# Softmax weights of a graph attention kept in PSUM for the products with values, and copied to SBUF by ScalarE

## The chip, the cores and the metric

The kernel runs on one core of a Trainium2 chip. The metric is device time in microseconds (us) of one execution; the time of a kernel is the median of several executions. A profile is taken of one further execution.

The engines are named as the profile names them: PE is TensorE (PEld its weight loads), DVE is VectorE, ACT is ScalarE, POOL is GpSimd, SP is SyncE.

## The reference, cut to what matters

The reference is two layers of a graph transformer on 3125 nodes and 100000 edges, sorted by destination. The change touches only the graph attention of the first layer:

```python
def _L0_gnn_ref(h, efeat, src, dst, Wq, Wk, Wv, W1, b1, W2, b2, Wo, bo):
    Q = (h @ Wq).reshape(n, H, HD)      # n = 3125 nodes, H = 8 heads, HD = 32
    K = (h @ Wk).reshape(n, H, HD)
    V = (h @ Wv).reshape(n, H, HD)
    score = jnp.einsum('ehd,ehd->eh', Q[dst], K[src]) / np.sqrt(HD)
    score = score + jax.nn.relu(efeat @ W1 + b1) @ W2 + b2
    m = jax.ops.segment_max(score, dst, num_segments=n)
    ex = jnp.exp(score - m[dst])
    denom = jax.ops.segment_sum(ex, dst, num_segments=n)
    alpha = ex / denom[dst]
    out = jax.ops.segment_sum(alpha[:, :, None] * V[src], dst, num_segments=n)
    return out.reshape(n, D) @ Wo + bo
```

The kernel subtracts a running maximum per head instead of the maximum per node, sums `ex * V[src]` and `ex` itself by destination, and divides at the end. Around it stand a dense mixer, a mixture of experts, a second graph layer, a second mixer and a feed-forward part, none of which is touched.

## The kernel before

**Tiling.** The 100000 edges are cut into 40 groups (`NG`) of 2500: four runs (`NR`) of five columns (`KB`) with 125 edges each, one edge per partition. So one group has 20 columns (`GT`). Each run has a buffer `KV` of 125 partitions, five columns and 521 floats per column: 256 for the keys, 256 for the values, eight for the weights `ex`, one constant 1. There are ten such buffers, used in turn, so that the gathers can run up to two and a half groups ahead.

**One group, in the order of the program.**

- POOL gathers the rows of `kv_tab` by source node, one indirect DMA for each column, 20 in a group (L901). SP loads the features of the edges two groups ahead, and the queries and codes of the group after.
- TensorE spreads the queries over the edges by a one-hot product, `qe` (L911). VectorE multiplies keys with it, in place (L914), and sums over each head to `sc` (reductions, L924). This is done for the first pair of runs (`z` = 0) and then for the second. Between these matmuls stand the hidden layer of the edge features of the next group (L783, evacuated by ScalarE at L785) and the output projection of the group before (L845 to L858).
- VectorE adds the bias of the edge features (L926) and finds the maximum: a reduction (L929), a transpose on TensorE (L934), a reduction (L936), a small matmul (L940), and the running maximum `top` (L942). It subtracts it (L944). Between the two matmuls TensorE does the scores of the next group (L796) into the PSUM tile `score`, which ScalarE copies out (L799), and counts (L835).
- ScalarE writes the exponentials into the last columns of each `KV` (L948), VectorE multiplies the values with them, in place (L950), and TensorE sums values and weights by destination, with a one-hot matrix `oh` as weights (L953):

```python
for z in range(2):
    for r in range(2 * z, 2 * z + 2):
        ex = kvs[r][:, :, 2 * D:2 * D + H]
        nc.scalar.activation(ex, sc[:, r * KB:(r + 1) * KB, :], AF.Exp)                                # L948
        v = kvs[r][:, :, D:2 * D].rearrange("p g (h d) -> p g h d", d=HD)
        nc.vector.tensor_tensor(v, v, ex[:, :, :, None].to_broadcast([P, KB, H, HD]), ALU.mult)        # L950
    for i in range(KB):
        for r in range(2 * z, 2 * z + 2):
            pe(nc.tensor.matmul(seg[r * W:(r + 1) * W, :], oh[:, r * KB + i, :], kvs[r][:, i, D:], ...))  # L953
```

  The four runs have four strips of 32 partitions of one PSUM tile `seg`.
- ScalarE copies `seg` to SBUF as `u` (L715), a matmul moves its rows to their window (L719), and ScalarE copies the result as `U` (L971). VectorE adds what the group before carried over (L958 to L975, with an exponential of eight elements at L961) and divides (L979 to L988). TensorE turns the features of the group after the next (L772, copied out by ScalarE at L774), and the next group begins.

**What sets the order.** Every matmul of this stage is tied to the one before by `pe(...)`, so TensorE runs in the order of the program. On the other engines the tile framework orders by priorities and by the dependencies between tiles. It places the waits: an instruction waits for the engines that last wrote or used its tiles. On VectorE the one-hot matrix `oh` of the next group (L697) comes right after the four products, and it waits for the segment sums.

**PSUM.** The eight banks are all in use in this stage: two for `tr` (small transposes and matmuls), two for `hidden`, two for `qe`, one for `score` and one for `seg`.

Of the kernel before, what the change touches and what calls it, by code (L numbers as in the profile page):

```python
# [9 lines left out]
F32 = mybir.dt.float32  # L10
BF16 = mybir.dt.bfloat16
I32 = mybir.dt.int32
AF = mybir.ActivationFunctionType
# [4 lines left out]
N, E, D, H, FE = 3125, 100000, 256, 8, 64  # L18
HD = D // H
P, T = 125, 25  # L20
# [14 lines left out]
NG, NR, KB = 40, 4, 5  # L35
GT = NR * KB
# [41 lines left out]
def kernel(ctx: ExitStack, tc: tile.TileContext, a, out):  # L78
    nc = tc.nc
# [37 lines left out]
    def row(t, shape):  # L117
        return t[:, None, :].to_broadcast(shape)
# [603 lines left out]
    with tc.tile_pool(name="l1", bufs=1) as l1, tc.tile_pool(name="l2", bufs=2) as l2, \  # L722
# [30 lines left out]
        def pe(x):  # L753

            if before[0] is not None:
                tc.add_manual_dep(x.ins, before[0], NOSYNC, reason="order of matmuls")
            before[0] = x.ins.name
# [117 lines left out]
        for g in range(NG):  # L875
# [15 lines left out]
            sc = l2.tile([P, GT, H], F32, name="sc")  # L891
            kvs = []
# [49 lines left out]
            nc.vector.tensor_max(top, old, tps[:, :H])  # L942
            tops.append(top)
            nc.vector.tensor_sub(sc, sc, row(top[:P], [P, GT, H]))  # L944
            for z in range(2):
                for r in range(2 * z, 2 * z + 2):
                    ex = kvs[r][:, :, 2 * D:2 * D + H]
                    nc.scalar.activation(ex, sc[:, r * KB:(r + 1) * KB, :], AF.Exp)  # L948
                    v = kvs[r][:, :, D:2 * D].rearrange("p g (h d) -> p g h d", d=HD)
                    nc.vector.tensor_tensor(v, v, ex[:, :, :, None].to_broadcast([P, KB, H, HD]), ALU.mult)  # L950
                for i in range(KB):
                    for r in range(2 * z, 2 * z + 2):
                        pe(nc.tensor.matmul(seg[r * W:(r + 1) * W, :], oh[:, r * KB + i, :], kvs[r][:, i, D:],  # L953
                                            start=i == 0, stop=i == KB - 1))
# [64 lines left out]
    with tc.If(nc.values_load(flag[0:1, 0:1], min_val=0, max_val=1)):  # L1019
        with tc.tile_pool(name="qp", bufs=1) as qp:  # L1020
# [171 lines left out]
            with tc.tile_pool(name="y1", bufs=1) as l1, tc.tile_pool(name="y2", bufs=2) as l2, \  # L1192
# [14 lines left out]
                with tc.For_i(0, n, 1):  # L1207
                    bi = block_indices(l2, step)
                    nc.vector.tensor_scalar_add(step, step, 1.0)
                    for t in range(T):  # L1210
# [12 lines left out]
                        sc = l2.tile([P, G, H], F32, name="sc")  # L1223
# [11 lines left out]
                        ex = l2.tile([P, G, H], F32, name="ex")  # L1235
# [70 lines left out]
    with tc.tile_pool(name="f1", bufs=1) as f1, tc.tile_pool(name="f2", bufs=2) as f2, \  # L1306
# [96 lines left out]
        for e in range(NE):  # L1403
# [20 lines left out]
            for (s0, ns), xe in zip(SUB, xes):  # L1424
# [8 lines left out]
                r = f2.tile([128, D], F32, name="yr", bufs=3)  # L1433
# [23 lines left out]
    with tc.tile_pool(name="m1", bufs=1) as m1, tc.tile_pool(name="m2", bufs=2) as m2, \  # L1457
# [3 lines left out]
        for g in range(0, T, 5):  # L1461
            r = slice(g, g + 5)
# [86 lines left out]
    with tc.tile_pool(name="h1", bufs=1) as h1, tc.tile_pool(name="h2", bufs=2) as h2, \  # L1549
# [245 lines left out]
        def small(name, dt=F32, shape=(128, 1)):  # L1795
            return h1.tile(list(shape), dt, name=name)

        digits = [(25, 128), (18, 128), (11, 128), (4, 128), (0, 16)]
        part = small("part", I32)
# [74 lines left out]
        for g in range(5):  # L1874
            r = slice(5 * g, 5 * g + 5)
# [47 lines left out]
```

## Time and profile before

| | us |
|---|---|
| median of 3 runs | 2893.51 (2891.22 to 2893.81) |
| the profiled execution: time | 2897.13 |
| the profiled execution: span, first to last instruction | 2895.3 |
| stage of the edge groups, first product (L950) to the end of its work | about 416 to 1706 |

In the stage from 416 to 1706 us, of 1290 us, the engines are busy:

| engine | us |
|---|---|
| PE | 1000.67 |
| DVE | 966.17 |
| ACT | 448.68 |
| POOL | 1014.11 |

The granted clock of TensorE is 0.91 of full speed in this stage, and the DMA engines are busy for 0.81 of it, at 186 GB/s.

How to read it: a group of instructions is given by line, engine, operation and tiles (out<-in), with its count, its busy time, the mean of one in ns, the idle time of the engine just before it, and what ended most of that idle time. In a timeline, equal neighbours are merged (x4), start and length are in us, and the brackets hold idle time and what ended it. PEclk is the share of full speed that the throttle granted to TensorE. No engine is busy for the whole of the stage, so the busy times alone do not say what sets the pace.

### The profile page before, as it was taken

What the parts mean: (1) busy time and instruction counts of PE and PEld (TensorE: products, weight loads), DVE (VectorE), ACT (ScalarE), POOL (GpSimd) and SP (SyncE); (2) the same over time, 40 slices, a digit from 0 to 9 for tenths busy, and PEclk for the clock granted to TensorE, in tenths of its full rate; (3) what the DMA queues carried; (4) which work ended last, traced back from release to release, by engine and by line L of the source; (5) the groups of instructions that cost most, each with busy time, mean ns of one, the idle gap of its engine ahead of it and who ended that gap; (6) DMA issues with size and microseconds to landing.
All of it is one profiled execution on the core that took longest, in us unless ns stands there. A gap on an engine that the chain in (4) does not pass through costs nothing. (4 is left out here: it accounts for less than half of the span.)

```text
span 2895.3 us, 40359 instructions
## 1 busy us (share of the span) xinstructions
PE 2240.8 (77%) x14013; PEld 1404.5 (49%) x14013; DVE 1875.0 (65%) x4137; ACT 934.7 (32%) x1838; POOL 1364.6 (47%) x1172
## 2 busy tenths in 40 slices
PE   2588777777777777787777744799689999978894
PEld 1244434444444444444444323465457775756673
DVE  4748337777777777777777658343478844846446
ACT  0243133333333333333333304212163323243331
POOL 3444368888888887788888712211100002221110
PEclk9788869999998999989999866899899999999997
DMA  7740488888888888888888842233200002000001
GB/s 187 159 126 17 109 192 191 183 193 190 188 193 190 187 195 187 190 188 189 191 194 191 184 111 85 79 98 105 55 2 5 5 1 70 2 1 1 1 19 48
DMA packets 272347, 340.23 MB, mean 118 GB/s; under 512 B 156170, under 2 KB 203437, under 8 KB 271534
## 3 DMA queue, kind: packets, MB, share of 16 engines
q0 software_dynamic: 185600, 219.53, 33.4%
q1 hardware_dynamic: 72794, 101.95, 13.5%
q10 hardware_dynamic: 13732, 16.01, 2.2%
q8 instruction: 114, 1.87, 0.3%
q14 instruction: 107, 0.88, 0.1%
HBM read 294.80 MB, written 43.25 MB: 117 GB/s over the span
## 5 line engine op out<-in xcount | busy, mean ns | idle before, releaser
L901 POOL DMA_INDIRECT KV<-kv_tab,srcs x800 | 1077.4, 1347 | 330.2 <-issue 148.9
L914 DVE TENSOR_TENSOR KV<-KV,qe 125x512 f32<-125x512 f32 (+1 forms) x480 | 266.3, 595 | 154.9 <-PE qe L911 142.9
L953 PE MATMUL seg<-KV,oh 125*32 125x265 f32 x1600 | 267.6, 525 | 126.3 <-DVE KV L950 115.6
L785 ACT ACTIVATE hid<-hidden,b1e 128x910 f32<-128x910 f32 (+1 forms) x240 | 249.5, 1039 | 304.0 <-PE hidden L783 304.0
L911 PE MATMUL qe<-q,ohT 64*125 64x256 bf16 x2400 | 220.2, 280 | 98.5 <-DVE KV L914 95.5
L911 PEld LDWEIGHTS <-ohT 64*125 64x125 bf16 x2400 | 159.7, 134 | 218.3 <-issue 210.8
L783 PE MATMUL hidden<-efT,w1e 64*128 64x455 f32 (+1 forms) x960 | 240.3, 574 | 16.1 <-ACT hid L785 14.7
L953 PEld LDWEIGHTS seg<-KV,oh 125*32 125x32 f32 x1600 | 133.0, 143 | 244.7 <-DVE KV L950 160.8
L924 DVE TENSOR_REDUCE sc<-KV 125x40 f32<-125x1280 f32 x160 | 229.9, 1478 | 0.0
L950 DVE TENSOR_TENSOR KV<-KV 125x1280 f32<-125x1280 f32 x160 | 227.9, 1487 | 1.5 <-ACT KV L948 1.4
L1493 PE MATMUL sum<-adj,f 125*128 125x400 bf16 (+1 forms) x1050 | 197.2, 328 | 0.0
L1295 PE MATMUL build<-oc,op 128*125 128x200 bf16 x1176 | 144.0, 262 | 55.9 <-ACT xn L214 41.4
L192 DVE TENSOR_TENSOR op<-values,ends_of 128x756 bf16<-128x756 bf16 x196 | 108.3, 553 | 93.4 <-PE build L1295 91.5
L1295 PEld LDWEIGHTS <-op 128*125 128x125 bf16 x1176 | 125.8, 144 | 82.3 <-ACT xn L214 41.5
L1493 PEld LDWEIGHTS <-f 125*128 125x128 bf16 x1200 | 115.7, 98 | 102.9 <-issue 31.2
L192 DVE TENSOR_TENSOR oc<-values,ends_of 128x1200 bf16<-128x1200 bf16 x196 | 152.3, 777 | 0.0
L1562 POOL DMA_DIRECT2D ln_cols<-in_L_mix_ln_g_dram x1 | 0.8, 787 | 316.3 <-DVEq L1513 316.3
L1298 ACT ACTIVATE adj<-build 125x400 bf16<-125x400 f32 x171 | 86.0, 504 | 186.0 <-PE build L1295 186.0
L715 ACT ACTIVATE u<-seg 128x265 f32<-128x265 f32 x40 | 15.7, 393 | 332.3 <-PE seg L953 332.3
L1619 PE MATMUL mm<-bt,fw 128*128 128x250 f32 (+1 forms) x416 | 100.8, 405 | 26.4 <-DVE bt L110 23.3
L265 PE MATMUL mm<-bt,w 128*128 128x489 f32 x256 | 110.5, 582 | 5.1 <-ACT bt L112 3.3
L265 PE MATMUL mm<-w,hT 128*128 128x256 f32 (+1 forms) x512 | 112.6, 379 | 0.0
(462 smaller groups left out, 3910.4 us busy)
## 6 DMA issues: line engine op xcount, KB each, us to landing
EF<-in_edge_attr_dram SPq DMA_DIRECT2D x40, 625.0 KB
w<-in_L_ffn_w_dram SPq DMA_DIRECT2D x16, 1024.0 KB
KV<-kv_tab,srcs POOLq DMA_INDIRECT x800
q<-q_tab SPq DMA_DIRECT2D x160, 48.0 KB
dlb<-dl_tab SPq DMA_DIRECT2D x160, 39.1 KB
kv_tab<-kvt SPq DMA_DIRECT2D x25, 224.0 KB
o_tab<-ow SPq DMA_DIRECT2D x40, 128.0 KB
q_tab<-q SPq DMA_DIRECT2D x25, 168.0 KB
```

Source lines behind the costliest of these rows:

```text
L192: nc.vector.tensor_tensor(dst.rearrange("p n (m o) -> p n m o", o=2), values.rearrange("p (u m o) -> p u m o", u=1, o=2).to_broadcast([dst ...
L265: nc.tensor.matmul(o, l, r, start=i == 0, stop=i == len(pairs) - 1)
L783: pe(nc.tensor.matmul(ps[:, s, :n * F2], w1e[f, c * 128:(c + 1) * 128], efTs[g][f, p0:p0 + n, :], start=True, stop=True))
L785: nc.scalar.activation(hids[g][:, c, p0:p0 + n, :].rearrange("h p (f s) -> h s p f", s=2), ps[:, :, :n * F2].rearrange("h s (p f) -> h s p ...
L901: nc.gpsimd.indirect_dma_start(out=kv[:, i, :2 * D], out_offset=None, in_=kv_tab, in_offset=indirect(srcs[:, e:e + 1]))
L911: pe(nc.tensor.matmul(ps[:, i, :], ohT[w, z, (i0 + i) * P:(i0 + i + 1) * P], q3[w, z, k, :], start=k == 0, stop=k == 2))
L914: nc.vector.tensor_mul(kv[:, i0:i0 + nt, :D], kv[:, i0:i0 + nt, :D], ps[:, :nt, :])
L924: nc.vector.tensor_reduce(sc[:, r0:r0 + KB, :], kv[:, :, :D].rearrange("p g (h d) -> p g h d", d=HD), AX.X, ALU.add)
L950: nc.vector.tensor_tensor(v, v, ex[:, :, :, None].to_broadcast([P, KB, H, HD]), ALU.mult)
L953: pe(nc.tensor.matmul(seg[r * W:(r + 1) * W, :], oh[:, r * KB + i, :], kvs[r][:, i, D:], start=i == 0, stop=i == KB - 1))
L1295: pe(nc.tensor.matmul(ps[:, j // CT, :], op[:, j, :P], oc[:, j, :], start=j % CT == 0, stop=j % CT == CT - 1))
L1493: pe(nc.tensor.matmul(sps[c][:, :n], f3[:, t, i, c * 128:(c + 1) * 128], adj[:, t, :n], start=t == 0 and i == 0, stop=t == T - 1 and i == 2))
```

## The change

One PSUM tile named `score`, of the same size and in the same bank as the scores of the edge features, takes the exponentials of the group. ScalarE makes them in two instructions of 80 columns instead of four of 40, one ahead of each pair of runs. VectorE's product reads them from PSUM. Behind each product in the program, ScalarE copies the run's 40 columns from PSUM to the place in `KV` where the segment matmuls read them. Everything else keeps its place.

```diff
             nc.vector.tensor_sub(sc, sc, row(top[:P], [P, GT, H]))
+
+            exps = pl.tile([128, 3, P], F32, name="score")[:P].rearrange("p a b -> p (a b)")
+            exps = exps[:, :GT * H].rearrange("p (j h) -> p j h", h=H)
             for z in range(2):
+                part = slice(2 * z * KB, 2 * (z + 1) * KB)
+                nc.scalar.activation(exps[:, part, :], sc[:, part, :], AF.Exp)
                 for r in range(2 * z, 2 * z + 2):
-                    ex = kvs[r][:, :, 2 * D:2 * D + H]
-                    nc.scalar.activation(ex, sc[:, r * KB:(r + 1) * KB, :], AF.Exp)
+                    ex = exps[:, r * KB:(r + 1) * KB, :]
                     v = kvs[r][:, :, D:2 * D].rearrange("p g (h d) -> p g h d", d=HD)
                     nc.vector.tensor_tensor(v, v, ex[:, :, :, None].to_broadcast([P, KB, H, HD]), ALU.mult)
+                    nc.scalar.activation(kvs[r][:, :, 2 * D:2 * D + H], ex, AF.Copy)
                 for i in range(KB):
                     for r in range(2 * z, 2 * z + 2):
                         pe(nc.tensor.matmul(seg[r * W:(r + 1) * W, :], oh[:, r * KB + i, :], kvs[r][:, i, D:],
```

## The prediction

> **What bounds the kernel now.** The page comes first, because its slices show where this code runs (the graph attention of the first layer, slices 6 to 23) and its groups show what that stage is made of.
>
> ```profile
> span 2895.3 us, 40359 instructions
> L901 POOL DMA_INDIRECT KV<-kv_tab,srcs x800 | 1077.4, 1347 | 330.2 <-issue 148.9
> L953 PE MATMUL seg<-KV,oh 125*32 125x265 f32 x1600 | 267.6, 525 | 126.3 <-DVE KV L950 115.6
> L950 DVE TENSOR_TENSOR KV<-KV 125x1280 f32<-125x1280 f32 x160 | 227.9, 1487 | 1.5 <-ACT KV L948 1.4
> ```
>
> VectorE does 160 products with values (L950), four in each of 40 groups, and waits 1.5 us in all for exponentials. TensorE waits 115.6 us for these products before its segment sums (L953). The next question is whether a later product means a later group. The timeline of group 17 (one engine at a time) answers it:
>
> ```profile
> 966.50 0.31 DVE L944 TENSOR_TENSOR sc<-sc,top 125x160 f32<-125x160 f32 x1
> 966.84 0.62 ACT L948 ACTIVATE KV<-sc 125x40 f32<-125x40 f32 x4 [0.57 <-DVE sc L944]
> 967.11 5.70 DVE L950 TENSOR_TENSOR KV<-KV 125x1280 f32<-125x1280 f32 x4
> 968.66 0.78 PE L953 MATMUL seg<-KV,oh 125*32 125x265 f32 x2 [2.68 <-DVE KV L950]
> 970.06 4.55 PE L953 MATMUL seg<-KV,oh 125*32 125x265 f32 x33 [0.63 <-DVE KV L950]
> 975.32 0.39 ACT L715 ACTIVATE u<-seg 128x265 f32<-128x265 f32 x1 [7.77 <-PE seg L953]
> 975.32 0.82 DVE L697 TENSOR_TENSOR oh<-dl,iota 125x640 f32<-125x640 f32 x1 [2.51 <-PE seg L953]
> ```
>
> Four exponentials take 0.62 us, the products start behind the first of them and run without a gap, and then VectorE and ScalarE both stand until the segment sums are done. Nothing of the next group overtakes this. One group is a closed ring of legs, read from the same timeline: products 5.70; last product's end to the copy L715 2.51 at least; to the first query product (L914) 4.89; to the end of the first pair's reductions 7.49; of the second pair's 7.39; to the subtracted maximum (L944) 3.61; to the first product 0.30. Sum: 31.89 us. The measured pace is (1696.0 - 416.3)/39 = 32.81 us from the first product of the first group to that of the last. Over groups 1 to 37 the legs average 32.57, because the second one has a mean of 3.02 instead of 2.51. The rest is two late groups waiting for gathers: group 38 has a second pair's leg of 16.76, group 39 one of 8.86.
>
> Why the second leg varies is seen in stretches of the granted clock (columns: us, busy time and count of PE, PEld, DVE, ACT, POOL, then PEclk, DMA share, GB/s):
>
> ```profile
> 969.01:972.42 3.41, 2.78 (x14) 1.07 (x14) 3.41 (x3) 0.00 (x0) 3.11 (x2) 0.50 0.91 187
> 972.43:999.70 27.27, 21.72 (x197) 12.39 (x193) 20.06 (x46) 11.71 (x23) 21.30 (x19) 1.00 0.88 187
> 999.73:1006.55 6.82, 5.59 (x29) 2.67 (x31) 5.07 (x4) 0.00 (x0) 5.91 (x4) 0.50 0.86 195
> 1006.56:1033.86 27.30, 20.72 (x184) 11.77 (x179) 20.81 (x46) 11.70 (x23) 22.11 (x18) 1.00 0.86 202
> ```
>
> TensorE idles during the products, and its clock is halved for 3.41 or 6.83 us; it returns for 27.3 us. All these are multiples of 3.413 us, and every edge of the stage lies on one fixed grid of that step. A long half-clock stretch still covers the last product's segment matmuls: ten passes at 0.22 us, or at 0.44 us. Each us of overlap adds half a us to the leg (2.51 without overlap, 3.28 and 4.12 seen).
>
> The gathers are the other candidate:
>
> ```profile
> 967.70 1.96 POOL L901 DMA_INDIRECT KV<-kv_tab,srcs  x1 [0.30 <-issue]
> 969.97 2.51 POOL L901 DMA_INDIRECT KV<-kv_tab,srcs  x1 [0.30 <-issue]
> 972.78 1.18 POOL L901 DMA_INDIRECT KV<-kv_tab,srcs  x1 [0.30 <-PE seg L953]
> ```
>
> A gather's issue takes 1.2 us and a gap of 0.30, but 2.0 and 2.5 us while products run. Twenty of them need about 33.1 us per group, slightly more than the ring. They start far ahead (the last gather ends 55 us before its group's products) and have 17 us left by group 31. So they cost little until the end: about 0.9 us in each of four groups, and 9.4 + 1.5 us in groups 38 and 39. Together 14 us.
>
> **The change, part by part.**
> *Exponentials.* Four of 40 columns become two of 80. L961 (8 columns, 192 ns) and L948 (40 columns, 226 ns) give about 1 ns a column, so 0.26 us each: the first product starts 0.04 later. A write to PSUM by ScalarE is in no row; I take the same price (from 0.05 less to 0.1 more).
> *Products.* L950 takes its second input from PSUM. L914 does that already: 684 ns for 512 columns, 418 for 256, which is 1.04 ns a column and extrapolates to 1.48 us for 1280, against 1.487 now. Zero.
> *Copies and their waits.* This is the price. In the built program exps is one tile in the bank of "score", and each copy waits for the product just before it, each next product waits for the copy, and the second exponential waits for the second copy. VectorE's and ScalarE's readers of that tile take turns; they do not run side by side. The segment matmuls, which waited for products, now wait for copies. A copy of 40 columns from PSUM costs about 0.21 us (L808: 250 ns for 96 columns, 223 for 64), a handover 0.04 us (L944's end to the first product is 0.30, of which the exponential is 0.22: two handovers in 0.08). Products started every 1.40 us, overlapping their ends by 0.08. Now: product 1 to 2, 1.49 + 0.04 + 0.21 + 0.04 = 1.78, +0.38. Product 2 to 3 also has the exponential, + 0.04 + 0.26: +0.68. Product 3 to 4: +0.38. The last copy before its matmuls: +0.25. With the 0.04 at the start, D = 1.7 us per group, all of it on the ring: behind the waiting product on VectorE stand the other products and L697, which stood waiting for the segment sums anyway; behind the waiting copies on ScalarE stands L715, which does too. Bounds for D: 1.2 (handovers 0.02, ScalarE operations of 0.15) and 2.7 (handovers 0.1, operations of 0.3).
> *Elsewhere.* Order on TensorE, POOL and SP is the same, no DMA is added or moved. Six ScalarE operations instead of four are hidden in its idle time. The score tile of two groups on waits for the last copy, which is some 20 us old by then.
> *Clock.* D alone would give 31.89 + 0.07 (mean surplus of the sixth leg) + 1.7 = 33.66. But the matmuls now begin 3.6 us after the first product instead of 2.95 (the single pair before them apart), so a grid step has to start at 2.8 us or later to hold the 2.7 us of matmuls that a step held where half clock ended after it; nearly every group gets the 6.83 us stretch. Its end falls under the last strip by an amount that depends on where the grid lies, and each us costs half a us. As long as the group is shorter than ten steps (34.13 us), the grid edge falls later against the products in every next group, and the group grows, until it is 34.13 us and stays there. That holds for every D from about 0.6 to 2.2. So the pace is 34.13, and the exact D hardly matters.
> *Gathers.* With the products off their path they need about 31.1 us per group, with them in it still 33.1; both are below 34.13. So they run ahead as far as the ten KV buffers let them, and the 14 us of waits go.
> *Sum.* 38 intervals of 34.13 make 1296.9; the last, without features of a next group, 32.8 - 1.4 (its wait) + 1.7 = 33.1. Together 1330.0 against 1279.7: +50. The last group's own tail adds 1.7, the first groups, not yet on the grid, take off 1. **+51 us.** The profiled execution took 2897.13 us (2895.3 of span), which becomes 2948; the median of the runs, 2893.5, becomes **2944**.
>
> **Two rules of the skill.** The row: gathers of 2.0 to 2.5 us under L950 (two SBUF inputs), of 1.2 under L914 (one of them PSUM). The Trainium skill (SBUF — State Buffer, Who interferes with whom) says that a VectorE instruction with two SBUF inputs contends with a GpSimd instruction that reads SBUF, and that one with at most one doesn't. By it the gathers gain 2.1 us per group, and if they set the pace the sum would be a gain. Against the change speaks PSUM — Partial Sum Buffer (PSUM bank collisions): two engines must not be at the same bank and quadrant at once, reads included, so the copies cannot run beside the products. No row of this profile shows such a collision.
>
> **The rivals.**
> 1. Handovers through PSUM are dearer: D over 2.24. Then no slack of the grid is left, and the pace is 31.96 + D, at 2.7 34.66, +20 us more: up to 2964. For it: no row has ScalarE writing PSUM. Against: all its neighbours are cheap. 0.15.
> 2. The clock returns after one step, or sooner: pace 33.66, 38 x 0.47 = 18 us less, 2926. For it: 17 of the 40 groups have the short stretch now. Against: work begins later in every group. 0.12.
> 3. Faster: the gathers decide. If product and copy overlapped after all (D near 0), relieved gathers would give back their 14 us: 2879. It decides where D plus the clock's surplus (0.51 now) stays under 0.92, the gap of the pace 32.81 to the ring 31.89. For it: the slow gathers. Against: the waits in the program. 0.04. That the copies run "behind" the products is thus what the change would say and not do.
> 4. No difference, by the same balance at D about 0.4: 0.02.
>
> **Numbers.** The forecast has 0.67. The range takes in rivals 1 and 2 nearly whole: 2922 to 2962. A measurement here can tell about 0.2% (6 us) from no change. Slower 0.94, within 0.02, faster 0.04.
>
> **What would show it.** In the profile after: products 1.78, 2.08, 1.78 us apart instead of 1.40, with VectorE waiting for ScalarE at them; segment matmuls waiting for ScalarE; a group pace of 34.1 with half-clock stretches of 6.83; no gather over 1.5 us under the products; POOL waiting for segment sums; no long wait in groups 38 and 39. Products longer than 1.5 us, gaps between them under 0.1, or a pace under 33 would prove me wrong.

## The result, and the profile after

The changed kernel takes 2941.93 us (median of 4 runs, 2939.94 to 2946.96) against 2893.49: a ratio of 1.017, 95% interval [1.0153, 1.0187], 48 us slower. The profiled execution took 2943.4 us with a span of 2941.6, against 2897.13 and 2895.3.

The page of the changed kernel, cut to the groups that answer to those shown of before:

```profile
span 2941.6 us, 40361 instructions
L901 POOL DMA_INDIRECT KV<-kv_tab,srcs x800 | 995.0, 1244 | 429.3 <-PE seg L958 151.4
L958 PE MATMUL seg<-KV,oh 125*32 125x265 f32 x1600 | 313.2, 562 | 146.8 <-ACT KV L955 146.8
L954 DVE TENSOR_TENSOR KV<-KV,score 125x1280 f32<-125x1280 f32 x160 | 238.1, 1488 | 45.6 <-ACT score L950 23.8
L955 ACT ACTIVATE KV<-score 125x40 f32<-125x40 f32 x160 | 32.9, 206 | 243.7 <-DVE KV L954 243.7
```

A product takes 1488 ns, as before (1487): reading PSUM costs it nothing. What is new stands behind the second bar, in the waits. The products now wait 45.6 us for ScalarE, where it was 1.5; the copies (L955) wait for products, 243.7 us; the segment matmuls (L958) no longer wait for products, but for copies. The gathers are shorter, 1244 ns on the mean instead of 1347, and POOL now waits 151.4 us for segment sums: it has run ahead as far as the buffers allow.

The timeline of group 17, whose products begin at 990.41 us, shows the turns (cut to the lines that matter; POOL's stand behind the dots):

```profile
990.14 0.24 ACT L950 ACTIVATE score<-sc 125x80 f32<-125x80 f32 x1 [0.70 <-DVE f L965]
990.41 1.49 DVE L954 TENSOR_TENSOR KV<-KV,score 125x1280 f32<-125x1280 f32 x1
991.93 0.20 ACT L955 ACTIVATE KV<-score 125x40 f32<-125x40 f32 x1 [1.43 <-DVE KV L954]
992.17 1.49 DVE L954 TENSOR_TENSOR KV<-KV,score 125x1280 f32<-125x1280 f32 x1 [0.27 <-ACT KV L955]
994.20 1.49 DVE L954 TENSOR_TENSOR KV<-KV,score 125x1280 f32<-125x1280 f32 x1 [0.54 <-ACT score L950]
995.96 1.49 DVE L954 TENSOR_TENSOR KV<-KV,score 125x1280 f32<-125x1280 f32 x1 [0.27 <-ACT KV L955]
997.48 0.21 ACT L955 ACTIVATE KV<-score 125x40 f32<-125x40 f32 x1 [1.55 <-DVE KV L954]
1000.80 0.39 ACT L715 ACTIVATE u<-seg 128x265 f32<-128x265 f32 x1 [3.11 <-PE seg L958]
...
993.57 1.18 POOL L901 DMA_INDIRECT KV<-kv_tab,srcs  x1 [2.94 <-PE seg L958]
995.34 1.20 POOL L901 DMA_INDIRECT KV<-kv_tab,srcs  x1 [0.58 <-PE seg L958]
996.84 1.19 POOL L901 DMA_INDIRECT KV<-kv_tab,srcs  x1 [0.30 <-PE seg L958]
```

Products start 1.76, 2.03 and 1.76 us apart instead of 1.40, with a copy, or a copy and an exponential, between any two. Gathers that run under products take 1.2 us.

The granted clock in stretches of the same profile (PEclk is the number behind the last bracket):

```profile
992.19:998.96 6.77, 6.10 (x28) 2.37 (x30) 4.45 (x3) 0.86 (x4) 4.20 (x4) 0.50 0.49 127
998.97:1026.26 27.29, 20.65 (x181) 11.41 (x177) 20.52 (x45) 11.55 (x21) 20.92 (x17) 1.00 0.86 198
1026.31:1033.10 6.79, 6.11 (x28) 2.37 (x30) 4.46 (x3) 0.86 (x4) 3.59 (x4) 0.50 0.56 130
1033.12:1060.40 27.28, 20.64 (x181) 11.40 (x177) 20.33 (x45) 11.57 (x21) 20.59 (x17) 1.00 0.86 191
```

Each of groups 0 to 38 has a half-clock stretch of two steps at its products, and from group to group the clock drops exactly ten steps later, 34.13 us, all 38 times. In the kernel before these drops are nine steps apart 17 times, ten 20 times and once, at the late group, 13. From group 17 to 23 each group's products begin 1.75 us ahead of the clock's drop, to 0.01 us. Group 24 begins 0.26 us late and so stands only 1.50 us ahead; in the two groups behind it is 1.63 and 1.69 us: the loop creeps back to its place on the grid. The mean pace is (1740.6 - 411.6)/39 = 34.08 us; it was 32.81.

### The profile page after: what moved, and what is told of

It reads as the page before. It is cut to its first block, busy times and chain, and to the rows that moved or that the text cites. A ratio compares the mean times of both kernels' runs of the same rounds, so it can differ in the third digit from the quotient of the medians.

```text
span 2941.6 us, 40361 instructions
## 1 busy us (share of the span) xinstructions
PE 2280.5 (78%) x14013; PEld 1388.3 (47%) x14013; DVE 1888.2 (64%) x4137; ACT 963.3 (33%) x1918; POOL 1284.6 (44%) x1172
## 3 DMA queue, kind: packets, MB, share of 16 engines
q0 software_dynamic: 185600, 219.53, 32.7%
## 5 line engine op out<-in xcount | busy, mean ns | idle before, releaser
L901 POOL DMA_INDIRECT KV<-kv_tab,srcs x800 | 995.0, 1244 | 429.3 <-PE seg L958 151.4
L958 PE MATMUL seg<-KV,oh 125*32 125x265 f32 x1600 | 313.2, 562 | 146.8 <-ACT KV L955 146.8
L958 PEld LDWEIGHTS seg<-KV,oh 125*32 125x32 f32 x1600 | 121.1, 148 | 322.6 <-ACT KV L955 186.6
L954 DVE TENSOR_TENSOR KV<-KV,score 125x1280 f32<-125x1280 f32 x160 | 238.1, 1488 | 45.6 <-ACT score L950 23.8
L955 ACT ACTIVATE KV<-score 125x40 f32<-125x40 f32 x160 | 32.9, 206 | 243.7 <-DVE KV L954 243.7
L697 DVE TENSOR_TENSOR oh<-dl,iota 125x640 f32<-125x640 f32 x40 | 33.0, 825 | 124.1 <-PE seg L958 124.0
```

The lines of the kernel that those rows point to most:

```text
L901: nc.gpsimd.indirect_dma_start(out=kv[:, i, :2 * D], out_offset=None, in_=kv_tab, in_offset=indirect(srcs[:, e:e + 1]))
```

## The experiments

Some versions only place or order the same work differently. Others add work: e1 makes the exponentials twice, e4 and e5 repeat copies, and the fill matmuls compute something that nobody reads. D is, as in the prediction, the time that a version's waits add to a group. The versions were run in three sets, each on one chip and beside the kernel before. The chips differ in one thing that matters here: on those of the first two sets the sixth leg of a group (last reduction to subtracted maximum) is longer, on the mean 4.3 to 4.4 us instead of 3.7. So times are compared within a set, and legs are read from each trace. This is the table of all traces (means over groups 1 to 37, us; "behind" is the leg from the last product's end to the copy L715; the pace is that from the first group to the last):

| version | pace | sixth leg | products | behind | mean gather, ns | ratio to before |
|---|---|---|---|---|---|---|
| before (first profile) | 32.81 | 3.68 | 5.70 | 3.02 | 1347 | |
| the change | 34.08 | 3.67 | 7.04 | 3.28 | 1244 | 1.017 |
| *first set* | | | | | | |
| e1_exps_twice | 33.50 | 4.38 | 5.68 | 3.22 | 1262 | 1.0012 |
| e2_sbuf_turns | 33.26 | 4.42 | 5.70 | 3.05 | 1359 | 1.000 |
| e3_one_exp | 34.47 | 4.38 | 6.77 | 3.13 | 1244 | 1.014 |
| e5_three_copies | 36.26 | 4.34 | 8.48 | 3.33 | 1257 | 1.038 |
| *second set* | | | | | | |
| b_before_again | 33.27 | 4.42 | 5.70 | 3.11 | 1357 | |
| a_after_again | 34.48 | 4.32 | 7.04 | 3.00 | 1262 | 1.0162 |
| w_after_filled | 34.32 | 4.30 | 7.16 | 2.77 | 1240 | 1.0151 |
| w_e1_filled | 32.82 | 4.34 | 5.68 | 2.54 | 1268 | 0.9951 |
| *third set* | | | | | | |
| w_before_filled | 32.70 | 3.37 | 5.70 | 2.51 | 1347 | 0.9976 |
| w_e1_filled_again | 31.69 | 3.28 | 5.68 | 2.53 | 1235 | 0.9842 |
| e8_pairs | 33.98 | 3.64 | 6.20 | 4.00 | 1261 | 1.0153 |
| e4_one_more_copy | 34.14 | 3.66 | 7.28 | 3.08 | 1233 | (one run) |

**e1_exps_twice.** The products keep PSUM, the copies go: ScalarE computes the weights a second time, from SBUF. The edit against the kernel before, cut:

```diff
+            exps = pl.tile([128, 3, P], F32, name="score")[:P].rearrange("p a b -> p (a b)")
+            exps = exps[:, :GT * H].rearrange("p (j h) -> p j h", h=H)
+            nc.scalar.activation(exps, sc, AF.Exp)
...
-                    ex = kvs[r][:, :, 2 * D:2 * D + H]
-                    nc.scalar.activation(ex, sc[:, r * KB:(r + 1) * KB, :], AF.Exp)
+                    ex = exps[:, r * KB:(r + 1) * KB, :]
...
+                    nc.scalar.activation(kvs[r][:, :, 2 * D:2 * D + H], sc[:, r * KB:(r + 1) * KB, :], AF.Exp)
```

> One exponential of 160 columns goes to PSUM for the products; ScalarE makes the weights in KV by four exponentials of 40 columns from sc, as in the kernel before, so no instruction of ScalarE reads the PSUM tile and nothing takes turns. Theory of turns: products again 1.40 us apart, D about 0.1 (the longer first exponential), gathers at 1.2 us under the products, so pace 31.96 + 0.1 + a clock surplus of about 0.5 = 32.5 and no gather waits in the late groups: about 2880, some 14 us faster than before. Rival 'PSUM is dear by itself' (products or exponentials slower from or to PSUM): slower than before, over 2910.

Measured: 2916.74 us against 2914.21, ratio 1.0012 [0.9992, 1.0032]. Who the products waited for, in this version (the view of one line, cut):

```profile
L954 DVE TENSOR_TENSOR KV<-KV,score x160: 1478/1481/1490, 413.4 to 1724.1; 125x1280 f32<-125x1280 f32 x160
  ACT score L948: 2.3, 4
```

With no instruction of ScalarE reading that tile, the products run without a gap again, 1.40 us apart, out of the same PSUM, and the loss is gone. PSUM is not dear by itself; the turns were. The 14 us of gain did not come. The trace of the unchanged kernel on such a chip (b_before_again, below) says why: there the gathers' lead, the time from the end of a group's last gather to its first product, is still 33.5 us in group 36, where it was 16.9 in the first profile, and group 38 doesn't wait, so there was no wait to take away. On a chip with short sixth legs this version ran only with the fill.

**e2_sbuf_turns.** Two exponentials, four products, four copies as in the change, but written over `sc` in SBUF: `exps = sc`.

> The change with its exponentials in SBUF (written over sc) instead of PSUM; the same two exponentials, four products and four copies. Theory of turns: in the built program the copies no longer wait for the products, only the exponentials; products 1.40 us apart, segment matmuls wait for products, gathers again 2.0 to 2.5 us under the products: the time of before within 8 us (2886 to 2902). Rival 'the copies cost, wherever they read': near the changed kernel, 2935 or more.

Measured: 2912.66 us, ratio 1.000 [0.9984, 1.0016]. Products 1.40 us apart, gathers under them 2.25 us on the mean again (PSUM versions: 1.19). The copies themselves cost nothing where they need no turns: here ScalarE stands in front of none of the 160. So the program makes the two readers of the PSUM tile wait for each other, but not the two readers of this SBUF tile; that an instruction waits for the engines that last used its tiles, as is said ahead of the prediction, is too wide.

**e3_one_exp.** One exponential of 160 columns in place of two, all copies and turns kept.

> The change with one exponential of 160 columns in place of two of 80, so that the wait between the second and third product is shorter by the exponential and one handover (0.28 us) and the first product 0.07 us later: D 1.47 instead of 1.67. Theory of the clock grid: the pace stays at 34.13 us per group (ten steps of 3.413) and the time at that of the changed kernel within 3 us (2939 to 2945); the clock's surplus grows by 0.2 us instead. Rival 'the waits add up simply': pace 33.9, 8 us less, 2934.

Measured: 2955.56 us, ratio 1.014 [1.0112, 1.0169]; the changed kernel on a chip with as long a sixth leg has 1.0162 [1.0144, 1.018]. Products 1.76 us apart throughout. The wait saved (D of 1.44 by its legs, against 1.64 of the change) is not seen in the pace, 34.47 against 34.48: the leg behind the products is 0.13 longer, the sixth leg, on another chip, 0.06. But with a sixth leg of 4.38 the ring alone is at 34.1, so this does not yet show the grid; e8 does.

**e5_three_copies.** Each copy made three times.

> The change with every copy made three times over (same data): each further copy of a run adds about 0.24 us (0.205 and a wait for the copy before), 8 in a group: D 1.67 + 1.9 = 3.6, past the 2.2 us up to which the grid gives slack. Theory of turns with the grid: pace 31.96 + 3.6 = 35.6 with no or little clock surplus, 38 x 1.45 = 55 us more than the changed kernel, about 2998. Rival 'waits add up simply on today's pace': 38 x 1.9 = 72 us more, 3014. Rival 'copies run behind, off the ring': no change, 2942.

Measured: 3024.88 us, ratio 1.038 [1.0353, 1.0406]. The legs give a D of 3.56 (products 2.78 longer, the last copies 0.72, the first exponential 0.06), and the pace 36.26 is the ring of this chip, about 32.7, plus that. So beyond the slack a wait costs nearly its full length: 1.92 us more D than in a_after_again, below, and 1.78 us more pace. Less is left for the clock: the leg behind exceeds its floor, the leg at full clock, of 3.23 by 0.10, where b_before_again has 0.60. In time it is 63 us more than a_after_again (the kernel before took 2914 us on that chip too), between the 55 of the theory and the 72 of the rival 'waits add up simply', so this run does not part these two; it does rule out copies that run off the ring.

**b_before_again and a_after_again.** Both kernels unchanged, in the second set.

> The kernel before, unchanged, for its trace on the chip of this set. The versions with the exponentials made twice or kept in SBUF showed a sixth leg (last reduction to subtracted maximum) of 3.6 to 5.3 us, mean 4.4, where the trace of before had 3.68. If that is the chip, this trace shows it too on the same chip; if it belongs to those versions, this trace has 3.7 again.

> The changed kernel, unchanged, beside the others of this set. Theory of the clock grid: on a chip where the other legs are as in the first trace, the pace is 34.1 us; where the sixth leg is 0.8 us longer, the ring alone is 31.89 + 0.8 + 1.67 = 34.4, no slack of the grid is left, and the pace is about 34.5 to 34.7. In both cases 1.4% to 1.8% slower than before on the same chip.

The kernel before took 2904.71 us in the one run with its trace (2914.61 in the median of the runs beside the others), the changed one 2962.25. The sixth leg of the unchanged kernel is 4.42 here: it is the chip, not the versions. In its waits VectorE stands before L836, up to 2.5 us after the counts that L836 reads (L835) are done, 31 us in all; the first profile has none of this. The operations named in the view are not what L836 needs; they are those that ended last before it:

```profile
DVE deg L836 <- PE tr L934: 18.7, 23, 1.2
DVE deg L836 <- PE score L796: 11.0, 6, 2.5
```

What holds it was not found. The change costs 1.0162 [1.0144, 1.018] here, as much as on the first chip, with a pace of 34.48: the ring of 32.7 + 1.64 = 34.3 is past ten steps, and the clock's surplus, what the leg behind takes over its floor, is down to 0.25 us.

**w_after_filled.** The change, with 13 matmuls in TensorE's idle time.

```diff
+            fills = pl.tile([128, 512], F32, name="tr", bufs=2)
+            for _ in range(13):
+                pe(nc.tensor.matmul(fills, identb, ohT[:, 0, :512], start=True, stop=True))
             old, top = top, l2.tile([128, H], F32, name="top", bufs=4)
```

> The changed kernel with 13 matmuls of 512 columns in TensorE's idle time between the maximum's matmul and the segment matmuls; nobody reads their result. Theory: this keeps TensorE busy enough that its clock is not halved, or only for one step, the second leg falls to its floor (2.5 to 2.8 us) in most groups, and the pace leaves the grid: 31.96 + 1.67 = 33.6 where the legs are as in the first trace (34.1 without the fill), so about 18 us less than the changed kernel beside it; D stays. Rival 'the waits alone make the time': no change by the fill, within 5 us. Rival 'the fill gets in the way': slower than the changed kernel.

Measured: 2958.6 us, beside 2962.25 of the unfilled one: 3.7 us, inside the spread of either. From the first group's first product to the last group's, half clock falls from 300 to 62 us, and the leg behind falls to its floor, as expected; but that leg had only 0.25 us over its floor on this chip, and the products' leg grew by 0.12 (why is not known). The 18 us were forecast for a chip with short legs. By its time alone this run fits the rival 'the waits alone make the time', and the fill was not tried with the change where the sixth leg is short.

**w_e1_filled.** The version with the exponentials made twice, with 12 such matmuls.

> The version with the exponentials made twice (one of 160 columns to PSUM for the products, four of 40 to KV), with 12 such matmuls. Theory: no turns (products 1.40 us apart), gathers relieved (1.2 us under the products), and no clock loss: ring 31.96 + 0.1 = 32.1 with the legs of the first trace, 32.9 with a sixth leg 0.8 us longer; against before on the same chip 0.5 to 0.8 us a group less, 20 to 30 us faster (ratio about 0.991). Rival 'relief of the clock is nil': ratio 1.000, as without the fill.

Measured: 2898.67 us against 2914.61, ratio 0.9951 [0.9935, 0.9968]. That is 16 us of the 20 to 30 expected. Against b_before_again the leg behind falls from 3.11 to 2.54, by more than the whole gain in pace, 0.45 us; the longer first exponential takes 0.14 back.

**w_before_filled and w_e1_filled_again.** They share the fill, and differ in where the products take the weights from.

> The kernel before, with nothing in PSUM changed, and 12 fill matmuls ahead of its segment matmuls. Together with the filled version of the exponentials made twice, on the same chip, it tells what relieving the gathers is worth. Theory: nothing, as long as the gathers have a lead left; the fill alone takes the clock's surplus (0.5 to 0.6 us a group) away: pace 32.7 where before has 33.3, ratio about 0.993, within 0.2% of the filled version with the exponentials made twice. On a chip where before itself waits for gathers in its last groups (about 14 us), the gathers at 33.1 us a group fall behind a ring of 32.0 and hold it, and the other filled version is 15 to 25 us faster. Rival 'the gain of that version was the gathers': here ratio 1.000.

> The filled version with the exponentials made twice, again, beside the filled version of before. Ratio 0.995 as before, 0.991 if this chip lets before wait for its gathers. See there for what the difference of the two tells.

Measured: 2891.51 us, ratio 0.9976 [0.9964, 0.9988], and 2848.9 us, ratio 0.9842 [0.9823, 0.9861]. The chip has short sixth legs, and the two are 43 us apart, where 15 to 25 were expected. VectorE's waits for gathers, first in the filled version of before, then POOL's wait for buffers in the other:

```profile
DVE KV L914 <- DMA KV<-kv_tab,srcs: 26.7, 22, 9.2
DVE KV L914 <- issue: 8.3, 4, 2.9
```

```profile
POOL KV L901 <- PE seg L960: 64.1, 154, 3.1
```

With the fill the ring of before is 31.56 or 31.57 us in most of the first 15 intervals, its gathers take 33.3 a group (groups 16 to 36), and from group 16 on they hold it: its second pair's leg is 7.39 to 7.49 in groups 1 to 15, mostly 8 to 10 and up to 11.25 after, and 18.00 in group 38. With the products out of the gathers' way the ring runs at 31.7 to the end, and POOL waits for buffers instead. So relief of the gathers was worth nothing where the ring itself took 33.3 us or more (e1), and 1 us per group where the ring was faster than the gathers. This version beats both kernels: 48 us under before, in the set with short legs.

**e8_pairs.** One exponential, as in e3; the copies of a pair behind both of its products. The edit of the copies, cut:

```diff
             for r in range(2 * z, 2 * z + 2):
                 nc.vector.tensor_tensor(v, v, ex[:, :, :, None].to_broadcast([P, KB, H, HD]), ALU.mult)
-                nc.scalar.activation(kvs[r][:, :, 2 * D:2 * D + H], ex, AF.Copy)
+            for r in range(2 * z, 2 * z + 2):
+                nc.scalar.activation(kvs[r][:, :, 2 * D:2 * D + H], exps[:, r * KB:(r + 1) * KB, :], AF.Copy)
```

> The change with one exponential of 160 columns, and with the two copies of a pair behind both of its products: one turn in the middle instead of three, D = 0.13 (longer exponential) + 0.47 (middle) + 0.34 (two copies at the end) = 0.94 instead of 1.67. Theory of the clock grid: the pace is 34.1 us all the same, on a chip with short sixth legs (ring 32.9) as on one with long ones (ring 33.65), because the clock's surplus grows to fill the ten steps; so nearly the whole cost of the change stays, 1.2% to 1.6% slower than before. Rival 'waits add up simply': 0.73 us a group less than the changed kernel, pace 33.4 (short legs) or 33.75 (long ones).

Measured: 2941.01 us against 2897.29, ratio 1.0153 [1.0136, 1.017]: the cost of the change nearly unmoved, with 0.67 us less of waits in every group. The timeline of its group 17:

```profile
990.52 2.88 DVE L953 TENSOR_TENSOR KV<-KV,score 125x1280 f32<-125x1280 f32 x2
993.84 2.88 DVE L953 TENSOR_TENSOR KV<-KV,score 125x1280 f32<-125x1280 f32 x2 [0.43 <-ACT KV L955]
1000.85 0.83 DVE L697 TENSOR_TENSOR oh<-dl,iota 125x640 f32<-125x640 f32 x1 [4.13 <-PE seg L958]
```

and the granted clock around it:

```profile
992.92:999.72 6.80, 5.96 (x33) 3.95 (x35) 3.37 (x3) 0.60 (x4) 3.66 (x4) 0.50 0.55 144
999.75:1027.03 27.28, 19.93 (x177) 11.18 (x173) 21.47 (x46) 11.45 (x20) 21.61 (x17) 1.00 0.83 194
1027.06:1033.85 6.79, 5.95 (x33) 3.93 (x35) 3.37 (x3) 0.60 (x4) 3.65 (x4) 0.50 0.52 143
```

Counted from their start, the products end 0.84 us earlier than in the change (996.72 against 997.45, from a start 0.11 later), and the segment sums are done no earlier: VectorE waits 4.13 us for them instead of 3.35. The clock comes back at 999.7, 3.0 us after the last product, where it came at 999.0, 1.5 us after it. Group after group starts 34.13 us behind the other (groups 13 to 21: 34.12 to 34.14).

**e4_one_more_copy.** One of the four copies made twice.

> The change with the copy of the first run made twice: D 1.67 + 0.24 = 1.91. Theory of the clock grid: on a chip with short sixth legs the ring is 33.87, still under ten steps, and the pace stays at 34.1; on one with long legs there is no slack left and the pace is 0.2 us over that of the changed kernel (34.48), 34.7. Rival 'waits add up simply': 0.24 us more on either.

Measured: 2950.12 us, one run; the pace from the trace is 34.14. With 0.24 us more of waits than the change, the median group is 34.12 us long, and the leg behind is 0.20 shorter.

## Why the prediction was right

**The place.** It said that the loss stands in the turns on one PSUM bank, on a ring that nothing overtakes. e1 (no turns, same PSUM) and e2 (same copies, no PSUM) each take the loss away, and e5 makes it larger by nearly what it adds.

**The sizes.** Spacings of 1.76, 2.03 and 1.76 us stand against 1.78, 2.08 and 1.78; the exponential of 80 columns took 0.241 us (0.26 forecast), the copy 0.205 (0.21), a product 1.488 (1.48). ScalarE's write to PSUM, for which no row gave a price, was no dearer: the same exponential of 80 columns takes 0.261 us to SBUF in e2. By the legs D is 1.34 in the products, 0.06 before them and 0.24 behind them, 1.64 against 1.7.

**The clock grid.** A pace of 34.13 us for every D from 0.6 to 2.2 was the boldest step. It held at the three D that were tried on chips with short sixth legs, by the legs' means:

| | D | surplus behind the products | sum | median group |
|---|---|---|---|---|
| e8_pairs | 0.97 | 4.00 - 2.85 = 1.15 | 2.12 | 34.11 |
| the change | 1.64 | 3.28 - 2.75 = 0.53 | 2.17 | 34.10 |
| e4_one_more_copy | 1.88 | 3.08 - 2.75 = 0.33 | 2.21 | 34.12 |

(The second number of each difference is the leg at full clock: before's 2.51 and the copies behind the last product.) What the waits don't take of ten steps, the half clock does. The bound of the slack showed too: with a ring about 0.7 us longer, a_after_again leaves the grid, and five of its drops come eleven steps after the one before.

On one point the forecast of the two-step stretches was lucky. The prediction said that a step must hold about 2.7 us of matmuls to end half clock, and left the pair of matmuls that runs ahead of the rest out of the count. In the trace that pair is in the step. The step of before with the least matmul time that ended half clock, and the first step of the change's group 22, which did not end it (PE busy is the second number):

```profile
1525.39:1528.80 3.41, 2.72 (x15) 1.16 (x18) 3.41 (x3) 0.00 (x0) 2.80 (x3) 0.50 0.55 155
1162.83:1166.24 3.41, 2.72 (x10) 0.91 (x12) 2.86 (x2) 0.45 (x2) 1.43 (x2) 0.50 0.59 177
```

At its place on the grid the change stood at the edge, with no margin that a trace can tell; and the edge is not sharp, for in b_before_again a first step of 2.78 us ended half clock and one of 2.86 did not. The second rival, the clock back after one step and 18 us less, was nearer than its 0.12 says. In most groups of e8 and e4 the first step holds 2.56 us or less, so there the stretch of two steps is safe.

**The gathers.** Relieved as expected, 1.19 us under the products instead of 2.23; their lead in group 36 is 49 us instead of 17, and group 38's second pair's leg fell from 16.76 to 7.39. A second wait was misread: group 39's leg of 8.86 stayed, in every version. It is no wait for gathers; in the last group TensorE has no hidden layer to do, and its clock is halved in that leg in every trace. The term of 1.4 us, taken off for it, was wrong: the last interval took 33.75 us instead of 33.1.

**The sum.** The stage took 1329.0 us from the first group's first product to the last group's, against 1330.0 forecast. That the two agree so closely is in part luck: the first 38 intervals took 1295.3 instead of 1296.9, which hides the last one's error. The total moved by 48 us between medians where 51 were forecast, and by 46 between the profiled executions: in the profile after, the first group's products begin at 411.6 us instead of 416.3, ahead of all that was changed. That start lay anywhere from 407 to 417 us in these traces, at 407.4 in another one of the unchanged kernel, so it is no part of the change.

**The rivals.** Dear handovers fell with D at 1.64. A clock back after one step fell with the stretches: two steps in groups 0 to 38. The gathers as the bound fell in e1: relieved gathers brought nothing there. Their price, 14 us, was the value for a ring of before's length on a chip where it waits for them. At a ring of 31.7 us the same relief brought 43.

**The two rules.** Gathers of 2.2 us under products with two SBUF inputs and 1.19 under those with one from PSUM agree with the Trainium skill (SBUF — State Buffer, Who interferes with whom); as the sum said, this did not set the pace here. A copy beside a product on the same bank, against which PSUM — Partial Sum Buffer (PSUM bank collisions) warns, was not tried: in all versions they take turns, by waits that stand in the program, or don't meet. So no run shows what the chip would do without these waits.

## What to carry to other kernels

Before an operand is moved to relieve one engine, look at what else reads it there: two engines that read one PSUM tile took turns, by the waits of the program, and each turn stood in a ring of work that had no slack, while the engine that was relieved was not the one that set the pace. Close the ring first, leg by leg, in the trace; a relief pays only when the ring is shorter than what was relieved, and here that took a second change, the fill. Where a TensorE clock is halved in the gaps of a loop, saved or added waits may not show in the time at all, so read the legs and not only the time.

## What the runs showed of the hardware

Not expected in this size: a loop can be held at a multiple of the clock's steps. With D of 0.97 and 1.64 us the clock's drops are ten steps of 3.413 us apart from group 0 to group 38 without exception, with 1.88 us in all but the first interval. A group that comes late is made up for by the groups behind it; apart from the first six and the last two, single groups are 33.9 to 34.5 us long, and the median is 34.10 to 34.12.

Twelve idle-time matmuls of 512 columns per group took half clock, from the first group's first product to the last group's, from 259 to 19 and 18 us in the version with the exponentials made twice (each on another chip), and shortened its leg behind the products from 3.22 to 2.54 and 2.53 us. The sixth leg is also 0.3 us shorter with them on the chip with short legs (3.28 against 3.61 in the median); the cause is not known.

A VectorE product of 1280 columns with both inputs in SBUF stretched the issue of a gather under it from 1.19 to 2.25 us on the mean (e2 against e1, on one chip); with one input from PSUM it did not.

Chips differ by nearly half of what this change costs: the same unchanged kernel took 2893 us on the chip of the first profile, and 2914, 2915 and 2897 on those of the three sets. The slower two have a longer sixth leg, in which VectorE starts an instruction up to 2.5 us after everything that the profile shows it to need, 31 us in all in b_before_again. Its cause stays open. That the kernel is only some 20 us slower there is in part because group 38 then doesn't wait for gathers.
